# Layer 3's token layer: gate weights without their mean, and tokens scaled by the identity that transposes them

## The chip, the cores and the metric

The kernel runs on one core of one Trainium2 chip. The metric is the device time of one execution in microseconds; three executions of the kernel before gave 7714.85 (median), 7708.21 and 7727.53. The engines are named as in the profile: PE (TensorE matmul), PEld (TensorE weight load), DVE (VectorE), ACT (ScalarE), POOL (GpSimd) and SP (SyncE, which issues DMAs).

## The reference

Four layers run one after the other on an array of 8 images of 56x56 pixels with 128 channels: a deformable convolution block, a whitening, and two token layers, each an attention and a mixture of experts. Only the way into the experts of layer 3 (the fourth) matters here. It takes the tokens after the linear attention, 3136 per image, normalizes each over its 128 channels, multiplies by 64 rows of gate weights, and picks for every expert the eight tokens with the highest softmax over the tokens:

```python
def _ln_t(v, eps=1e-5):
    m = jnp.mean(v, axis=-1, keepdims=True)
    s = jnp.var(v, axis=-1, keepdims=True)
    return (v - m) / jnp.sqrt(s + eps)
...
t = t + _L3_attn_ref(_ln_t(t), L3_attn_w_in, L3_attn_w_out, L3_attn_b_out, L3_attn_ln_w)
t = t + _L3_ffn_ref(_ln_t(t), L3_ffn_gate_w, L3_ffn_gate_b, L3_ffn_weight1, L3_ffn_weight2)
...
# in _L3_ffn_ref
logits = jnp.einsum('bsd,ed->bse', x, gate_w) + gate_b
probs = jax.nn.softmax(logits, axis=1)
vals, idx = jax.lax.top_k(probs.transpose(0, 2, 1), K)
```

## The kernel before

The layers follow each other in one program. Nearly all of the span belongs to the convolution, the whitening and layer 2's attention. Layer 3 has three parts: `context_sums` (a pass over all tokens for the attention's key sums), `linear_layer` (the rest of the attention, the gate and the choice of tokens) and `run_experts`. The change is in `linear_layer` and in `gate_weights`, which prepares the gate weights of layers 2 and 3 once, when the token layers begin.

**Tiling.** `linear_layer` cuts an image into 7 groups (NG) of 4 x 112 tokens (GT = 4, T = 112; QC = 448 tokens). Tokens lie on 112 partitions, 4 x 128 channels behind each other. A group is a Python generator, and each `yield` ends one of its stages. `pipeline` starts a new group each turn and advances every group in flight by one stage, so one turn holds one stage each of about ten different groups. There are 8 x 7 = 56 groups. Within a turn, a scheduler of the language settles the order of the instructions on each engine; every engine then works its own queue in order and waits where a semaphore says so.

**Stages of a group**, with the lines: load xT by DMA on SP (L2084); p_q = xT times w_in on PE (L2088) and its exponential q on ACT (L2101); sum m and reciprocal on DVE (L2103, L2104), q times m on POOL (L2105); transpose of q on PE (L121) and copy qT on ACT (L122); p_y on PE (L2112), its squares with sums sq on ACT (L2118), rs on DVE (L2122) and the power -1/2 on POOL (L2123); y on DVE (L2126) and t = t + y on POOL (L2129); then the normalization for the gate, which the change touches:

- `group_stats`: statistics and their aggregation on DVE (L1975, L1976), rs in `rsqrt`: add eps on DVE (L1140), power -1/2 on POOL (L1141);
- `minus_mean`: ms = -mean times rs on DVE (L1983); `scale_shift`: xn = t times rs + ms, four instructions on ACT (L1990);
- with the last group of an image, t goes to `t_c` and to the output by two DMAs on SP (L2138);
- `transpose_group`: four transposes of xn into PSUM tile p_tr on PE (L121), and a copy to nT on ACT (L122);
- p_g = gate weights times nT on PE (L2144), and pr = p_g + bias on ACT (L2145).

After an image's last group, `choose` goes on in the same generator: the top 8 of each row on DVE (L1650, L1653), exponentials on ACT (L1663), p_take on PE (L1679), four gathers from `t_c` issued on POOL (L1711), their statistics and p_pool (L1697 to L1706). These run in the turns of the next image's groups.

The identity `k.ident` is a constant 128x128 tile. A transpose takes the tile with the data as weights and the identity as the moving operand.

Of the kernel before, what the change touches and what calls it, by code (L numbers as in the profile page):

```python
# [8 lines left out]
F32 = mybir.dt.float32  # L9
# [3 lines left out]
ALU = mybir.AluOpType  # L13
AX = mybir.AxisListType
# [3 lines left out]
NB, IH, IW, C = 8, 56, 56, 128  # L18
S = IH * IW
T = 112  # L20
NT = S // T
GT = 4
# [24 lines left out]
E, HID, EG = 64, 512, 4  # L47
# [69 lines left out]
def transpose_group(nc, k, ps, tag, dst, src, copy):  # L117

    p = ps.tile([128, GT, T], F32, tag=tag, name="p_tr")
    for i in range(GT):  # L120
        nc.tensor.transpose(p[:, i, :], src[:, i, :], k.ident[:T, :T])  # L121
    copy(dst, p.rearrange("p a b -> p (a b)"))  # L122
# [889 lines left out]
def load_tokens(nc, dst, src):  # L1012

    nc.sync.dma_start(dst, src.rearrange("(t p) c -> p t c", p=T))
# [121 lines left out]
def rsqrt(nc, k, pool, mv, n):  # L1136

    m = mv.shape[0]
    rs = pool.tile([m, n], F32, name="rs")
    nc.vector.tensor_scalar(rs, mv[:, :, 1], EPS, None, ALU.add)  # L1140
    nc.gpsimd.tensor_tensor(rs, rs, k.mhalf[:m, :n], ALU.pow)  # L1141
    return rs
# [748 lines left out]
def pipeline(starts, every):  # L1891


    flight = []
    turn = 0
    starts = list(starts)
    while starts or flight:
        if starts and turn % every == 0:
            flight.append(starts.pop(0))
        advance(flight, len(flight))  # L1900
        turn += 1
# [68 lines left out]
def group_stats(nc, k, pool, x):  # L1970

    st = pool.tile([T, GT, 6], F32, name="st")
    mv = pool.tile([T, GT, 2], F32, name="mv")
    for i in range(GT):
        nc.vector.bn_stats(st[:, i], x[:, i])  # L1975
        nc.vector.bn_aggr(mv[:, i], st[:, i])  # L1976
    return rsqrt(nc, k, pool, mv, GT), mv


def minus_mean(nc, pool, rs, mv):  # L1980

    ms = pool.tile([T, GT], F32, name="ms")
    nc.vector.scalar_tensor_tensor(ms, mv[:, :, 0], -1.0, rs, ALU.mult, ALU.mult)  # L1983
    return ms


def scale_shift(nc, out, x, rs, ms):

    for i in range(GT):
        nc.scalar.activation(  # L1990
            out[:, i], x[:, i], AF.Identity, bias=ms[:, i : i + 1], scale=rs[:, i : i + 1]
        )
# [70 lines left out]
def linear_layer(tc, k, w, low, cw, t_in, xT_in, t_out, out, gate_w, gate_b, taken, pooled):  # L2063


    nc = tc.nc
    n_b = pooled.shape[1]
    G = GT * H3
    with ExitStack() as ctx:
        bp = ctx.enter_context(tc.tile_pool(name="llb", bufs=2))  # L2070
        wp = ctx.enter_context(tc.tile_pool(name="llw", bufs=3))
        ps = ctx.enter_context(tc.tile_pool(name="llp", bufs=8, space=PSUM))
        st_of = {}

        def group(n, g):
            if g == 0:
                t = bp.tile([T, NT, C], F32, name="t")
                load_tokens(nc, t, t_in[n])
                pr = bp.tile([E, S], F32, name="pr")
                st_of[n] = t, pr  # L2080
            t, pr = st_of[n]
            t = t[:, g * GT : (g + 1) * GT]
            xT = wp.tile([C, QC], F32, name="xT")
            nc.sync.dma_start(xT, xT_in[n][:, g * QC : (g + 1) * QC])  # L2084
            yield
            p = ps.tile([T, GT, C], F32, tag="m", name="p_q")
            for i in range(GT):
                nc.tensor.matmul(  # L2088
                    p[:, i], xT[:, i * T : (i + 1) * T], w.w_in[:, :C], start=True, stop=True
                )  # L2090
            q = wp.tile([T, GT, C], F32, name="q")
            q3 = q.rearrange("p a (h d) -> p (a h) d", d=D3)
            m = wp.tile([T, G], F32, name="m")
            mb = m.unsqueeze(2).to_broadcast([T, G, D3])
            if low is None:
                p3 = p.rearrange("p a (h d) -> p (a h) d", d=D3)
                nc.vector.tensor_reduce(m, p3, AX.X, ALU.max)
                nc.vector.tensor_tensor(q3, p3, mb, ALU.subtract)
                nc.scalar.activation(q, q, AF.Exp)
            else:  # L2100
                nc.scalar.activation(q, p, AF.Exp, bias=low[:T])  # L2101
            yield
            nc.vector.tensor_reduce(m, q3, AX.X, ALU.add)  # L2103
            nc.vector.reciprocal(m, m)  # L2104
            nc.gpsimd.tensor_tensor(q3, q3, mb, ALU.mult)  # L2105
            yield
            qT = wp.tile([C, QC], F32, name="qT")
            transpose_group(nc, k, ps, "m", qT, q, nc.scalar.copy)
            yield
            p = ps.tile([T, GT, C], F32, tag="m", name="p_y")  # L2110
            for i in range(GT):
                nc.tensor.matmul(  # L2112
                    p[:, i], qT[:, i * T : (i + 1) * T], cw, start=True, stop=True
                )
            y = wp.tile([T, GT, C], F32, name="y")
            sq = wp.tile([T, GT], F32, name="sq")
            for i in range(GT):
                nc.scalar.activation(  # L2118
                    y[:, i], p[:, i], AF.Square, accum_out=sq[:, i : i + 1]
                )  # L2120
            rs = wp.tile([T, GT], F32, name="rs")
            nc.vector.tensor_scalar(rs, sq, 1.0 / C, EPS, ALU.mult, ALU.add)  # L2122
            nc.gpsimd.tensor_tensor(rs, rs, k.mhalf[:T, :GT], ALU.pow)  # L2123
            yield
            for i in range(GT):
                nc.vector.scalar_tensor_tensor(  # L2126
                    y[:, i], p[:, i], rs[:, i : i + 1], w.ln_w, ALU.mult, ALU.mult
                )
            nc.gpsimd.tensor_tensor(t, t, y, ALU.add)  # L2129
            yield  # L2130
            rs, mv = group_stats(nc, k, wp, t)
            yield
            ms = minus_mean(nc, wp, rs, mv)
            xn = wp.tile([T, GT, C], F32, name="xn")
            scale_shift(nc, xn, t, rs, ms)
            if g == NG - 1:
                for d in (t_out[n], out[n]):
                    nc.sync.dma_start(d.rearrange("(t p) c -> p t c", p=T), st_of[n][0])  # L2138
            yield
            nT = wp.tile([C, QC], F32, name="nT")  # L2140
            transpose_group(nc, k, ps, "m", nT, xn, nc.scalar.copy)
            yield
            p = ps.tile([E, QC], F32, tag="m", name="p_g")
            nc.tensor.matmul(p, gate_w, nT, start=True, stop=True)  # L2144
            nc.scalar.activation(  # L2145
                pr[:, g * QC : (g + 1) * QC], p, AF.Identity, bias=gate_b
            )
            if g == NG - 1:
                yield from choose(nc, k, wp, ps, pr, t_out[n], taken[:, n], pooled[:, n])

        pipeline([group(n, g) for n in range(n_b) for g in range(NG)], 1)


# [11 lines left out]


def gate_weights(nc, k, pool, rp, ps, gate_w, gate_b, name):
    raw = rp.tile([E, C], F32, name=name + "_raw")
    nc.sync.dma_start(raw, gate_w)
    p = ps.tile([C, E], F32, tag="tr", name="p_tr")  # L2170
    nc.tensor.transpose(p, raw, k.ident[:E, :E])
    t = pool.tile([C, E], F32, name=name)
    nc.vector.tensor_copy(t, p)
    b = pool.tile([E, 1], F32, name=name + "_b")
    with nc.allow_non_contiguous_dma(reason="one bias on each partition"):
        nc.sync.dma_start(b, gate_b.unsqueeze(1))
    return t, b


def token_layers(tc, k, a, y, out):  # L2180
# [3 lines left out]
    with ExitStack() as ctx:  # L2184
# [13 lines left out]
        with tc.tile_pool(name="tlr", bufs=1) as rp:  # L2198
            with tc.tile_pool(name="tlp", bufs=2, space=PSUM) as ps:
# [10 lines left out]
                for g in range(2):  # L2210
# [12 lines left out]
                w.w_out = transposed(nc, k, cp, rp, ps, a["L3_attn_w_out"], "w_out")  # L2223
                gates = [
                    gate_weights(
                        nc, k, cp, rp, ps, a[f"L{i}_ffn_gate_w"], a[f"L{i}_ffn_gate_b"], f"gate{i}"
                    )
# [116 lines left out]
```

## Time and profile before

| | |
|---|---|
| three executions | 7708.21, 7714.85, 7727.53 us |
| profiled execution, own time | 7718.14 us |
| its span on the core | 7716.3 us |
| mean granted TensorE clock | 0.90 |
| first and last t = t + y in `linear_layer` (start) | 7059.2 and 7435.5 us |
| busy in 7060 to 7440 us: PE, DVE, ACT, POOL | 259.0, 297.7, 283.9, 264.0 of 380 us |

The span is the time between the first and the last instruction on the core in the profiled execution; the time of the execution is 1.8 us longer. In the profile's lines a group of instructions is written as line, engine, operation, output<-inputs, shapes and count. In a timeline, each row has the start and the length in us; the brackets give the idle time of the engine just before, and what ended it. Times inside the span count from its start.

### The profile page before, as it was taken

To read this page: it belongs to the slowest core of one execution; us is meant where nothing else is said; L and a number is where in the kernel's file an instruction comes from. 1 tells how busy PE (TensorE), PEld (TensorE's weight loads), DVE (VectorE), ACT (ScalarE), POOL (GpSimd) and SP (SyncE) were. 2 spreads that over 40 slices of the span, in tenths; PEclk is the share of its full clock that TensorE was granted. 3 is DMA by queue.
4 is the path that set the end of the run, shared out by engine and by line. 5 is a ranking of instruction groups with operands and counts; after the bars stand their busy time and mean duration, and the time that the engine had idled before them with its cause. 6 is when DMAs were issued, how large, how long until landed. Compare 5 with 4: busy or idle time off the path is not lost. (4 is left out here: it accounts for less than half of the span.)

```text
span 7716.3 us, 157926 instructions
## 1 busy us (share of the span) xinstructions
PE 6482.3 (84%) x59883; PEld 2880.7 (37%) x59883; DVE 5284.8 (68%) x9856; ACT 4142.6 (54%) x6467; POOL 2935.1 (38%) x2555
## 2 busy tenths in 40 slices
PE   6659999556899999999999999999999997556654
PEld 4446666334233323323323323333333333245532
DVE  7975564366677777777777777777777776366752
ACT  4424444122666666666666666666666664056740
POOL 0011111022444444444444444444444443434653
PEclk8768898777999999999999999999999998788766
DMA  5453443376788778778778778778778775543543
GB/s 155 137 119 76 86 95 65 82 240 207 199 203 197 193 192 199 189 192 201 191 184 204 188 183 207 183 191 205 185 190 206 182 190 137 196 117 107 134 135 130
DMA packets 736303, 1287.38 MB, mean 167 GB/s; under 512 B 117698, under 2 KB 503108, under 8 KB 728516
## 3 DMA queue, kind: packets, MB, share of 16 engines
q1 hardware_dynamic: 725556, 1260.76, 65.1%
q0 software_dynamic: 6144, 12.60, 0.6%
q8 instruction: 484, 7.93, 0.5%
q10 hardware_dynamic: 3824, 3.68, 0.2%
q14 instruction: 295, 2.42, 0.1%
HBM read 286.04 MB, written 197.81 MB: 63 GB/s over the span
## 5 line engine op out<-in xcount | busy, mean ns | idle before, releaser
L1260 ACT ACTIVATE e<-p_s 128x768 f32<-128x768 f32 (+2 forms) x3712 | 2887.8, 830 | 1584.9 <-PE p_s L1252 1329.8
L1298 POOL COPY x<-sq 32x1152 f32<-32x1152 f32 x1792 | 2059.2, 1149 | 2067.6 <-PE p_s L1252 1330.0
L1271 DVE STREAM_TRANSPOSE sq<-e 128x768 f32<-128x768 f32 x2688 | 2434.5, 950 | 567.3 <-ACT e L1260 312.9
L1252 PE MATMUL p_s<-q,kT 32*128 32x384 f32 (+2 forms) x14848 | 1888.6, 548 | 33.6 <-ACT e L1260 18.6
L1305 PE MATMUL av<-e,va 128*32 128x384 f32 (+2 forms) x14848 | 1645.3, 515 | 30.4 <-DVE acc L1324 20.7
L1305 PE MATMUL avx<-x,va 128*32 128x384 f32 x10752 | 1138.3, 496 | 69.5 <-issue 40.2
L1252 PEld LDWEIGHTS p_s<-q,kT 32*128 32x128 f32 (+1 forms) x14848 | 654.8, 181 | 1252.6 <-issue 825.4
L1305 PEld LDWEIGHTS av<-e,va 128*32 128x32 f32 (+1 forms) x14848 | 294.5, 108 | 1049.4 <-issue 941.7
L1305 PEld LDWEIGHTS avx<-x,va 128*32 128x32 f32 x10752 | 353.2, 111 | 650.9 <-issue 595.2
L609 POOL TENSOR_TENSOR rs<-rs,mhalf 112x4 f32<-112x4 f32 x112 | 116.1, 1036 | 788.3 <-DVE rs L608 788.3
L1324 DVE TENSOR_TENSOR acc<-acc,avx 128x384 f32<-128x384 f32 x336 | 183.9, 547 | 229.9 <-PE avx L1305 228.6
L121 PE MATMUL p_tr<-ident,xn 112*128 112x112 f32 x672 | 134.6, 341 | 187.4 <-DVE xn L112 141.8
L1141 POOL TENSOR_TENSOR rs<-rs,mhalf 112x4 f32<-112x4 f32 (+2 forms) x136 | 168.1, 1236 | 269.3 <-DVE ntop L1942 123.8
L525 ACT COPY wT<-p_w 88x448 f32<-88x448 f32 x152 | 138.0, 922 | 194.1 <-PE p_w L523 161.4
L1990 ACT ACTIVATE xn<-t,ms,rs 112x128 f32<-112x128 f32 x448 | 185.3, 488 | 76.4 <-DVE ms L1983 76.4
L327 DVE SCALAR_TENSOR_TENSOR acc<-xp,dw,acc 128x3136 f32<-128x3136 f32 x56 | 194.3, 3478 | 31.3 <-ACT acc L322 31.2
L637 PE MATMUL p_f<-x1T,w 128*128 128x448 f32 x448 | 205.6, 583 | 4.4 <-DVE x1T L632 2.7
L121 PEld LDWEIGHTS p_tr<-ident,xn 112*128 112x128 f32 x672 | 98.7, 169 | 285.0 <-issue 185.1
L1385 POOL TENSOR_TENSOR rs<-rs,mhalf 128x3 f32<-128x3 f32 (+1 forms) x72 | 58.5, 815 | 365.0 <-DVE rs L1384 343.0
L523 PE MATMUL p_w<-ident,wide 112*88 112x112 f32 x896 | 146.5, 303 | 58.6 <-DMA px<-strips 34.1
L621 DVE TENSOR_TENSOR y<-y,p_rs 128x448 f32<-128x448 f32 x112 | 69.3, 619 | 176.6 <-PE p_rs L614 176.6
L122 ACT COPY xT<-p_tr 128x448 f32<-128x448 f32 x112 | 59.6, 532 | 229.8 <-PE p_tr L121 203.7
(354 smaller groups left out, 7830.9 us busy)
## 6 DMA issues: line engine op xcount, KB each, us to landing
x<-sq SPq DMA_DIRECT2D x5376, 144.0 KB
w<-in_L_ffn_weight_dram SPq DMA_DIRECT2D x64, 1024.0 KB
px<-strips SPq DMA_DIRECT2D x64, 616.0 KB
va_d<-va SPq DMA_DIRECT2D x16, 1600.0 KB
xT_d<-xT SPq DMA_DIRECT2D x112, 224.0 KB
xT<-xT_d SPq DMA_DIRECT2D x112, 224.0 KB
kT_d<-kT SPq DMA_DIRECT2D x16, 1568.0 KB
t<-t_a SPq DMA_DIRECT2D x16, 1568.0 KB
```

The source lines that it names most:

```text
L121: nc.tensor.transpose(p[:, i, :], src[:, i, :], k.ident[:T, :T])
L327: nc.vector.scalar_tensor_tensor(acc, xp[:, j // 3 : j // 3 + IH, j % 3 : j % 3 + IW], dw[:, j : j + 1], acc, ALU.mult, ALU.add,)
L523: nc.tensor.transpose(p[:, g], around[:, :, g], k.ident[:T, :T])
L637: nc.tensor.matmul(p, q.w1[:, f * 128 : (f + 1) * 128], x1T, start=True, stop=True)
L1141: nc.gpsimd.tensor_tensor(rs, rs, k.mhalf[:m, :n], ALU.pow)
L1252: nc.tensor.matmul(ss[j // 2][:m, j % 2, :width], kT[rows, 128 * i : 128 * i + m], q[rows, :width], start=True, stop=True,)
L1260: nc.scalar.activation(e[:m, 2 * j : 2 * j + 2, :width], ss[j][:m, :, :width], AF.Exp)
L1271: nc.vector.transpose(sq[:, :, i, j : j + 2].rearrange("p s j c -> p j s c"), exps[u, b, a, i][:, j : j + 2, :QB].rearrange("p j (s c) -> ...
L1298: nc.gpsimd.tensor_copy(*moves.pop(0))
L1305: nc.tensor.matmul(out, keys[u, b][1][:m, i, j, :], e[j], start=start, stop=stop)
L1324: nc.vector.tensor_tensor(to, to, in_order(av), ALU.add)
L1990: nc.scalar.activation(out[:, i], x[:, i], AF.Identity, bias=ms[:, i : i + 1], scale=rs[:, i : i + 1])
```

## The change

The normalized token is rs (t - mean). Its product with a gate row does not change when the mean of the gate row over the channels is taken off first, since the token without its mean sums to zero; and then the mean of the token need not be subtracted any more. So the gate rows lose their mean once, in `gate_weights` (for both layers), and in `linear_layer` xn is gone: the scale rs goes into the identity, as a diagonal tile `own` of 4 x 112 x 112, and a matmul of t with it scales and transposes at once. ms and xn are not computed any more; `own` is made on POOL; the four transposes become four ordinary matmuls with the weights t and the moving operand `own`, into p_n in place of p_tr. The DMAs of the last group move one stage up, and the number of stages stays as it was, by an empty `yield`.

```diff
             nc.gpsimd.tensor_tensor(t, t, y, ALU.add)
             yield
-            rs, mv = group_stats(nc, k, wp, t)
-            yield
-            ms = minus_mean(nc, wp, rs, mv)
-            xn = wp.tile([T, GT, C], F32, name="xn")
-            scale_shift(nc, xn, t, rs, ms)
+
+            rs, _ = group_stats(nc, k, wp, t)
+            own = wp.tile([T, GT, T], F32, name="own")
+            nc.gpsimd.tensor_tensor(
+                own,
+                k.ident[:T, :T].unsqueeze(1).to_broadcast([T, GT, T]),
+                rs.unsqueeze(2).to_broadcast([T, GT, T]),
+                ALU.mult,
+            )
             if g == NG - 1:
                 for d in (t_out[n], out[n]):
                     nc.sync.dma_start(d.rearrange("(t p) c -> p t c", p=T), st_of[n][0])
             yield
+            yield
             nT = wp.tile([C, QC], F32, name="nT")
-            transpose_group(nc, k, ps, "m", nT, xn, nc.scalar.copy)
+            p = ps.tile([C, GT, T], F32, tag="m", name="p_n")
+            for i in range(GT):
+                nc.tensor.matmul(p[:, i], t[:, i], own[:, i], start=True, stop=True)
+            nc.scalar.copy(nT, p.rearrange("p a b -> p (a b)"))
             yield
             p = ps.tile([E, QC], F32, tag="m", name="p_g")
             nc.tensor.matmul(p, gate_w, nT, start=True, stop=True)
...
     raw = rp.tile([E, C], F32, name=name + "_raw")
     nc.sync.dma_start(raw, gate_w)
+    mean = rp.tile([E, 1], F32, name=name + "_m")
+    nc.vector.tensor_reduce(mean, raw, AX.X, ALU.add)
+    nc.vector.tensor_scalar(mean, mean, 1.0 / C, None, ALU.mult)
+    nc.vector.tensor_scalar(raw, raw, mean, None, ALU.subtract)
     p = ps.tile([C, E], F32, tag="tr", name="p_tr")
     nc.tensor.transpose(p, raw, k.ident[:E, :E])
```

## The prediction

> **What bounds the kernel now.** I read the page's engine totals first.
>
> ```profile
> PE 6482.3 (84%) x59883; PEld 2880.7 (37%) x59883; DVE 5284.8 (68%) x9856; ACT 4142.6 (54%) x6467; POOL 2935.1 (38%) x2555
> ```
>
> POOL looks like the emptiest engine, but this is a mean over stages with different limits; almost all of the span is not touched by the change. So I went to the stage that is: `linear_layer` adds its 56 groups into t (L2129) from 7059.2 to 7435.5 us. The busy times by stretch of it (length; then PE, PEld, DVE, ACT, POOL busy and instructions; clock; DMA):
>
> ```profile
> 7060.00:7440.00 380.00, 259.01 (x1440) 189.21 (x1440) 297.66 (x1088) 283.92 (x963) 263.96 (x249) 0.80 0.46 121
> 7084.98:7090.35 5.37, 3.78 (x28) 2.74 (x28) 4.23 (x18) 4.91 (x17) 4.32 (x4) 1.00 0.15 44
> 7212.59:7223.30 10.71, 4.15 (x22) 3.95 (x22) 10.70 (x25) 4.97 (x17) 4.65 (x5) 0.66 0.02 6
> 7246.44:7257.21 10.77, 7.96 (x37) 5.74 (x38) 5.24 (x23) 7.18 (x27) 8.22 (x9) 0.68 0.87 227
> ```
>
> Here no engine is far from the others: a plain turn (row two), a turn with the top-8 search (three), one with the gathers (four). What closes a plain turn stands in POOL's timeline (start, length, idle before and who ended it):
>
> ```profile
> 7084.98 1.28 POOL L2129 TENSOR_TENSOR t<-t,y 112x512 f32<-112x512 f32 x1 [0.26 <-DVE y L2126]
> 7086.88 1.05 POOL L2105 TENSOR_TENSOR q<-q,m 112x512 f32<-112x512 f32 x1 [0.62 <-ACT xn L1990]
> 7088.10 1.02 POOL L2123 TENSOR_TENSOR rs<-rs,mhalf 112x4 f32<-112x4 f32 x1 [0.17 <-DVE rs L1140]
> 7089.09 1.01 POOL L1141 TENSOR_TENSOR rs<-rs,mhalf 112x4 f32<-112x4 f32 x1
> 7090.35 1.27 POOL L2129 TENSOR_TENSOR t<-t,y 112x512 f32<-112x512 f32 x1 [0.26 <-DVE y L2126]
> ```
>
> and DVE's, over the same turn:
>
> ```profile
> 7085.41 0.87 DVE L1983 SCALAR_TENSOR_TENSOR ms<-mv,rs 112x4 f32<-112x4 f32 x1
> 7086.29 0.29 DVE L1975 BATCH_NORM_STATS2 st<-t 112x6 f32<-112x128 f32 x1
> 7086.50 0.24 DVE L2104 RECIPROCAL m<-m 112x16 f32<-112x16 f32 x1
> ...
> 7087.56 0.39 DVE L2122 TENSOR_SCALAR rs<-sq 112x4 f32<-112x4 f32 x1
> 7087.87 0.16 DVE L1140 TENSOR_SCALAR rs<-mv 112x4 f32<-112x4 f32 x1
> 7089.15 1.13 DVE L2126 SCALAR_TENSOR_TENSOR y<-p_y,rs,ln_w 112x128 f32<-112x128 f32 x4 [1.13 <-POOL rs L2123]
> ```
>
> The loop is POOL t, DVE statistics of t, DVE reciprocal, POOL q, DVE rs, POOL rs, DVE y, POOL t: 5.37 us, of it POOL idle 0.26 + 0.62 + 0.17. Two readings matter. The 0.62 is put down to ACT, but the reciprocal that q needs ends at 7086.74, 0.14 before q starts, and it stands in DVE's queue behind the statistics, which need t. And ms takes 0.87 where the same line takes 0.16 in `context_sums` (6941.24): it starts at 7085.41 and ends 0.02 after POOL's t, so it sits out POOL's add; L2122 ends at 7087.95 with POOL's q (7087.93) likewise. ACT is not in the loop: xn waits for ms, and nothing in the loop waits for xn.
>
> Other turns are pure POOL, back to back, 4.40 us:
>
> ```profile
> 7066.18 1.02 POOL L2123 TENSOR_TENSOR rs<-rs,mhalf 112x4 f32<-112x4 f32 x1
> 7067.17 1.05 POOL L2105 TENSOR_TENSOR q<-q,m 112x512 f32<-112x512 f32 x1
> 7068.39 1.01 POOL L1141 TENSOR_TENSOR rs<-rs,mhalf 112x4 f32<-112x4 f32 x1 [0.17 <-DVE rs L1140]
> 7069.36 1.27 POOL L2129 TENSOR_TENSOR t<-t,y 112x512 f32<-112x512 f32 x1
> ```
>
> I sorted the 55 intervals between the adds by length: 9 near 4.4, 22 near 5.36, 7 near 10.4 (search), 6 near 10.8 (gathers), 11 mixed, of 6.1 to 8.4; together 376.3 us.
>
> **The change, part by part.** *ACT* loses four xn of L1990 per group, 1.65 us a turn; *DVE* loses ms, 0.87. Both are covered in the plain loop: the statistics behind ms wait for t in any case, which ends when ms does. I count no gain there.
>
> *PE* gets four ordinary matmuls for four transposes. In the trace a transpose is one record and a matmul two: four transposes into p_tr take 0.60, eight records of p_y 1.04, so at most 0.44 a turn at full clock and 0.9 at half. Cover: PE waits 1.59 us for q in a plain turn, and p_y, behind the new matmuls, feeds ACT's y, which now need not wait for 1.65 us of xn. Without cover it would be 55 x 0.44 = 24 us.
>
> *POOL* gets `own`, 56 multiplications of 112x448. No row has that shape. Bounds: at the rate alone of L1117 (128x3200 in 5.518 us, 1.72 ns an element) 0.77; the add L2129 as it stands, 1.26. Nearest is L2105, also a multiplication with one operand spread over the inner dimension: 1.05 less 64 elements at 1.72 ns is 0.94, which I take.
>
> The Trainium skill ("GPSIMD Engine Reference", section Elementwise — side-by-side cycle accounting) gives some 2.6 cycles an element at 1.2 GHz for two inputs; my estimate from it is 0.97, and the sum below would be 1 us higher. Its section Engine selection speaks against the change: it puts elementwise multiplication on VectorE, about twice as fast. The trace agrees only in part: DVE's `own` L1742, 128x512, takes 0.68 against POOL's 1.05.
>
> Where `own` stands: the built order has it directly behind L1141 and ahead of the next t in nearly every turn. Queued behind it is the add, on it the statistics, the reciprocal and q. In a plain turn the 0.26 before t goes, since y (1.13) is hidden under L1141 and `own` (0.97 + 0.94): 5.37 - 0.26 + 0.94 = 6.05, or +0.68. The 0.62 stays, for the reciprocal still stands behind the first statistics.
>
> - 9 POOL turns: +0.94 each, 8.5.
> - 22 plain turns: +0.68, 15.0.
> - 7 search turns: DVE is busy throughout (10.70 of 10.71), yet L1141 at the end releases t, and `own` comes between. Between -0.15 (ms there) and +0.94; the middle, +0.4: 2.8.
> - 6 gather turns: POOL's order of four gathers, rs, rs, t; +0.68: 4.1.
> - 11 mixed turns: between -0.87 (ms) and +0.68 plus; PE and DVE wait for the search's results, so I take little, +0.2: 2.2.
>
> Sum +32.6. *SP:* t_c and out are issued a turn earlier, past one xT load at most; PE waited 2.8 us in all for xT from 7060 to 7440. The earlier wait for the add is queued ahead of xT loads that have three buffers. Zero; without cover, those few us. *`gate_weights`:* six small DVE operations for both layers, at most 0.29 each (the copy of w_out), 1.7 us, with the PE transposes and DVE copies behind them. The cover is the load of t:
>
> ```profile
> 1602.02 0.48 DVE L1067 BATCH_NORM_STATS2 st<-t 112x6 f32<-112x128 f32 x2 [7.90 <-DMA t<-y]
> ```
>
> The profiled execution took 7718.14 (span 7716.3, 1.8 around it); with +32.6 it is 7750.7. It lies 3.3 above the median 7714.85, from which I forecast 7748.
>
> Ends: with 0.77 for `own` and the lower ends of search and mixed turns, 6.9 + 11.2 - 1.1 + 3.1 - 9.6 = +11; with 1.26 everywhere, 9 x 1.26 + 22 x 1.0 + 7 x 1.26 + 17 x 1.0 = +59.
>
> **Rivals.** *Hidden:* POOL is idle 116 of 380 us, and 56 x 0.94 = 53 fits. If the scheduler's new order closes the 0.62 gaps too, 22 plain turns cost 0.06 each and the sum is 32.6 - 13.6 = 19: 7734. Against it: the statistics remain ahead of the reciprocal.
>
> *POOL holds DVE more:* each `own` stops DVE's rs (L1140, L2122) as t stops ms now, and is as slow as an add: 7715 + 59 = 7774. For it: the 0.87. Against: ms itself is gone.
>
> *The long turns win:* in the 24 long turns DVE and ACT lie on the path, and each gets shorter by ms and xn, 0.87 + 1.65 = 2.5: -60, with +23.5 for the short ones -37: 7678. It decides from 1.0 us per long turn on (23.5 / 24). For it: DVE full in the search turns. Against: ms is only 0.15 there, and POOL's 8.22 of 10.77 with the gathers.
>
> **How the numbers follow.** A measurement of this kernel (7708.21 to 7727.53 unchanged) tells about 0.3%, 23 us. Forecast (+18 to +45) 0.60, hidden 0.17, holding 0.15, long turns 0.08. Slower by over 23: most of the forecast and all of holding, 0.68; the rest of the forecast, hidden and a part of the long turns, same 0.25; faster 0.07. The range leaves out the last rival and the top of the third: 7718 to 7772.
>
> **What would show it.** `own` near 0.94 with t directly behind it; plain turns near 6.05, POOL turns near 5.35; POOL's busy share in the stage above 0.8; ACT idle up. Wrong if q follows t without a gap, if `own` is under 0.6, or if the turns with search and gathers shrink by over 1 us.

## The result

| | median | lowest to highest | runs |
|---|---|---|---|
| kernel before | 7713.92 us | 7695.88 to 7727.53 | 11 |
| changed kernel | 7750.43 us | 7736.87 to 7763.54 | 11 |

The ratio is 1.0049, with a 95% interval of 1.004 to 1.0057: the change costs some 36 us. The profiled execution of the changed kernel took 7752.65 us (span 7750.6). Its engine totals, the first line of the page:

```profile
PE 6512.0 (84%) x60107; PEld 2913.0 (38%) x60107; DVE 5246.1 (68%) x9806; ACT 4067.8 (52%) x6243; POOL 2985.9 (39%) x2611
```

POOL gained 56 instructions and 50.8 us of busy time, ACT lost 224 instructions and 74.8 us, DVE lost 38.7 us; PE has 29.7 us more. One engine got more work and two got less, and the kernel is slower: the totals don't say why. So again the stage, from the first to the last start of t = t + y (L2129): 412.1 us, where it was 376.3. These +35.8 us agree with the 36.5 between the medians, so the rest of the program needs no look. Busy time by stretch (length; then PE, PEld, DVE, ACT, POOL with instructions; clock; DMA):

```profile
7060.00:7470.00 410.00, 285.42 (x1644) 218.88 (x1644) 251.93 (x1027) 211.76 (x747) 311.01 (x302) 0.81 0.42 110
7100.61:7106.61 6.00, 3.36 (x17) 2.83 (x16) 3.45 (x16) 1.98 (x11) 5.19 (x6) 0.68 1.00 273
7118.62:7130.81 12.19, 4.91 (x26) 3.79 (x25) 10.51 (x23) 2.92 (x12) 5.23 (x6) 0.69 0.13 36
```

POOL is busy for 311.0 of 410 us (0.76; before 264.0 of 380, 0.69), and DVE and ACT have fallen far behind it (0.61 and 0.52). The clock granted in the stage is what it was, 0.81 against 0.80. The second row is a plain turn, the third a turn that holds both long steps of a search (DVE busy for 10.51 of 12.19 us). Now POOL and DVE in that plain turn, from the timeline of all engines (start, length, idle before and what ended it):

```profile
7100.61 1.26 POOL L2129 TENSOR_TENSOR t<-t,y 112x512 f32<-112x512 f32 x1
7101.91 0.29 DVE L1975 BATCH_NORM_STATS2 st<-t 112x6 f32<-112x128 f32 x1 [2.31 <-POOL t L2129]
7102.12 0.23 DVE L2104 RECIPROCAL m<-m 112x16 f32<-112x16 f32 x1
...
7102.50 1.05 POOL L2105 TENSOR_TENSOR q<-q,m 112x512 f32<-112x512 f32 x1 [0.62 <-DVE mv L1976]
...
7103.65 1.02 POOL L2123 TENSOR_TENSOR rs<-rs,mhalf 112x4 f32<-112x4 f32 x1
7104.64 1.01 POOL L1141 TENSOR_TENSOR rs<-rs,mhalf 112x4 f32<-112x4 f32 x1
7104.70 1.12 DVE L2126 SCALAR_TENSOR_TENSOR y<-p_y,rs,ln_w 112x128 f32<-112x128 f32 x4 [1.06 <-POOL rs L2123]
7105.72 0.93 POOL L2134 TENSOR_TENSOR own<-ident,rs 112x448 f32<-112x448 f32 x1
7106.61 1.26 POOL L2129 TENSOR_TENSOR t<-t,y 112x512 f32<-112x512 f32 x1
```

Read it from the bottom. The next t (7106.61) follows `own` directly; y had been ready since 7105.82, so the old gap of 0.26 is gone and `own` sets the start. The 0.62 ahead of q is still there, because the reciprocal still stands behind the first statistics, and those wait for t. The turn is 6.00 us long, where it was 5.37. In the groups (count, then busy us and mean ns of one, then idle before), the first line is of the kernel before, from 7060 to 7440 us, the others of the changed kernel, whole execution:

```profile
L2129 POOL TENSOR_TENSOR t<-t,y 112x512 f32<-112x512 f32 x56 | 70.8, 1264 | 10.9 <-DVE y L2126 9.3 <-PE p_tr L121 1.3 <-DVE rs L1701 0.3
```

```profile
L2129 POOL TENSOR_TENSOR t<-t,y 112x512 f32<-112x512 f32 x56 | 70.8, 1265 | 3.2 <-DVE rs L2122 1.8 <-PE p_tr L121 1.3
...
L2134 POOL TENSOR_TENSOR own<-ident,rs 112x448 f32<-112x448 f32 x56 | 52.2, 932 | 4.1
```

`own` takes 0.932 us, 52.2 in all. POOL idles only 3.2 us ahead of the 56 adds and never for DVE's y, for which it idled 9.3 us before: nearly always the add waits for POOL itself. The turn shown is the one that was predicted, but not the commonest: only two of the 21 plain turns of the table below take 6.00. The others stand in the part on why the prediction was right.

### The profile page after: what moved, and what is told of

It is laid out like the page before. It is cut to its first block, busy times and chain, and to the rows that moved or that the text cites. A ratio compares the mean times of both kernels' runs of the same rounds, so it can differ in the third digit from the quotient of the medians.

```text
span 7750.6 us, 158188 instructions
## 1 busy us (share of the span) xinstructions
PE 6512.0 (84%) x60107; PEld 2913.0 (38%) x60107; DVE 5246.1 (68%) x9806; ACT 4067.8 (52%) x6243; POOL 2985.9 (39%) x2611
## 3 DMA queue, kind: packets, MB, share of 16 engines
q14 instruction: 295, 2.41, 0.1%
## 5 line engine op out<-in xcount | busy, mean ns | idle before, releaser
L1305 PE MATMUL av<-e,va 128*32 128x384 f32 (+2 forms) x14848 | 1644.4, 515 | 30.5 <-DVE acc L1324 20.7
L1141 POOL TENSOR_TENSOR rs<-rs,mhalf 112x4 f32<-112x4 f32 (+2 forms) x136 | 167.6, 1234 | 299.2 <-DVE rs L1140 130.4
L121 PE MATMUL p_tr<-ident,xn 112*128 112x112 f32 x448 | 91.8, 350 | 184.0 <-DVE xn L112 140.4
L327 DVE SCALAR_TENSOR_TENSOR acc<-xp,dw,acc 128x3136 f32<-128x3136 f32 x56 | 194.2, 3477 | 29.7 <-ACT acc L322 29.6
L1975 DVE BATCH_NORM_STATS2 st<-t 112x6 f32<-112x128 f32 x448 | 114.5, 276 | 101.6 <-POOL t L2129 100.5
L642 PE MATMUL p_f<-hid,w 128*128 128x448 f32 x448 | 180.2, 545 | 0.2 <-issue 0.2
```

What stands on the lines that cost most here:

```text
L327: nc.vector.scalar_tensor_tensor(acc, xp[:, j // 3 : j // 3 + IH, j % 3 : j % 3 + IW], dw[:, j : j + 1], acc, ALU.mult, ALU.add,)
L642: nc.tensor.matmul(p[:, :QC], q.w2[:, f], hid[:, f], start=(f == 0), stop=(f == 3))
L1305: nc.tensor.matmul(out, keys[u, b][1][:m, i, j, :], e[j], start=start, stop=stop)
```

## The experiments

The measure is the length of the stage from the first to the last start of the 56 adds, split by kinds of turn as in the prediction; each of the 55 intervals keeps the kind it had in the kernel before. One thing is counted otherwise: a search can spread over two turns, so each of the 7 search turns is taken together with the turn ahead of it (6 of the mixed and 1 of the plain ones), which leaves 21 plain and 5 mixed turns. The stage is a finer measure than the time, as the rest of the program varies: the first add starts between 7047.7 and 7072.1 us in the 14 profiled executions. But each stage is read from one execution. e8, whose edit lies outside the stage, came out 2.3 us below the kernel before, 2.1 of it in the mixed turns, so differences of some 3 us say nothing. The ratio is to runs of the kernel before on the same chip. In the diffs of the experiments the operands are written short, and only the lines that matter are given.

| kernel | stage | 9 POOL | 21 plain | 7 + 7 search | 6 gather | 5 mixed | median, ratio [95%] |
|---|---|---|---|---|---|---|---|
| before | 376.3 | 39.4 | 113.1 | 119.8 | 64.9 | 39.1 | 7713.92 |
| changed | 412.1 | 48.4 | 131.9 | 124.5 | 62.8 | 44.5 | 7750.43, 1.0049 [1.004, 1.0057] |
| e1 | 355.1 | 43.0 | 111.7 | 106.9 | 58.8 | 34.7 | 7707.34, 0.9982 [0.9971, 0.9993] |
| e2 | 361.6 | 39.4 | 112.8 | 117.2 | 61.6 | 30.5 | 7712.68, 0.9984 [0.9975, 0.9994] |
| e3 | 405.4 | 47.8 | 123.1 | 122.5 | 66.8 | 45.2 | 7757.07, 1.0039 [1.0027, 1.0051] |
| e4 | 358.7 | 39.4 | 112.9 | 110.1 | 60.2 | 36.1 | 7712.6, 0.9988 [0.998, 0.9997] |
| e5 | 391.7 | 48.4 | 122.8 | 119.7 | 58.6 | 42.2 | 7732.42, 1.0018 [1.0007, 1.0029] |
| e6 | 343.4 | 39.4 | 105.9 | 104.6 | 58.1 | 35.4 | 7695.03, 0.9966 [0.9953, 0.9979] |
| e7 | 429.9 | 55.9 | 143.4 | 131.6 | 61.8 | 37.2 | 7772.42, 1.007 [1.0053, 1.0086] |
| e8 | 374.0 | 39.4 | 113.1 | 119.7 | 64.7 | 37.0 | 7723.69, 1.0005 [0.9994, 1.0017] |
| e9 | 373.4 | 39.4 | 113.8 | 120.2 | 64.7 | 35.3 | 7712.02, 0.9999 [0.9988, 1.001] |
| e10 | 352.2 | 39.4 | 108.2 | 109.6 | 62.8 | 32.1 | 7689.71, 0.997 [0.9959, 0.9981] |
| e11 | 345.2 | 39.4 | 92.3 | 124.9 | 56.0 | 32.6 | 7683.07, 0.9963 [0.9951, 0.9975] |
| e12 | 336.7 | 43.5 | 105.3 | 105.6 | 57.9 | 24.5 | 7687.21, 0.9959 [0.9946, 0.9972] |

The kernel before stood at 7726.15 beside e1 to e4, at 7718.76 beside e5 to e8 and at 7711.96 beside e9 to e12.

### Where `own` is made: e1, e2, e3, e4

e1 makes `own` on DVE, one stage later:

```diff
-            nc.gpsimd.tensor_tensor(own, ident, rs, ALU.mult)
             yield
+            nc.vector.tensor_tensor(own, ident, rs, ALU.mult)
```

> The changed kernel with the multiplication that makes own on DVE, one stage later, in place of POOL; the four matmuls per group and the gate weights stay. Theory A (the 0.93 us of POOL per turn, queued ahead of t = t + y, is what the change costs): POOL has four instructions a turn again, plain turns go back to 5.4 us, the adds of the stage take 345 to 376 us in place of 412, and the time is 7685 to 7715. Theory B (the doubled PE work of the matmuls costs it): nothing of PE is changed, the stage stays at about 412 us and the time at 7750. Theory C (DVE pays as POOL did, since a DVE instruction here sits out POOL's add): the multiplication takes 0.9 to 1.3 us each and the time is 7730 to 7760.

The stage became 355.1 us, 57.0 shorter than the changed kernel's and 21.2 shorter than that of the kernel before. Theory A's numbers hold; theory C was right about the length of the multiplication, 1.151 us, and wrong about its price. DVE's part is dearer than its other rows: from L1742, at 0.68 for 512 elements, 0.60 would be my estimate for 448. Group and timeline of e1:

```profile
L2138 DVE TENSOR_TENSOR own<-ident,rs 112x448 f32<-112x448 f32 x55 | 63.3, 1151 | 24.8 <-POOL rs L1141 24.5
```

```profile
7089.29 1.27 POOL L2129 TENSOR_TENSOR t<-t,y 112x512 f32<-112x512 f32 x1
7089.36 1.69 DVE L2138 TENSOR_TENSOR own<-ident,rs 112x448 f32<-112x448 f32 x1
...
7090.52 1.40 POOL L2123 TENSOR_TENSOR rs<-rs,mhalf 112x4 f32<-112x4 f32 x1
```

DVE's `own` starts during POOL's add and ends 0.49 after it, and POOL's power behind it takes 1.40 instead of 1.02: the two engines stop each other. That held the gain down (the POOL turns are at 43.0, where they were at 39.4 before) but did not take it.

e2 makes `own` on ACT, in four instructions, also one stage later:

```diff
-            nc.gpsimd.tensor_tensor(own, ident, rs, ALU.mult)
             yield
+            for i in range(GT):
+                nc.scalar.activation(own[:, i], ident, AF.Identity, scale=rs[:, i:i+1])
```

> The changed kernel with own made on ACT, by four instructions per group that scale the identity by rs, where the four xn of L1990 were. Theory A: ACT does as before the change, POOL too, only ms is gone; plain turns 5.4 us, the stage 355 to 376 us, the time 7695 to 7715. Theory B (PE's matmuls): 412 us and 7750.

The stage is 361.6 us. The POOL and plain turns are back at 39.4 and 112.8, where the kernel before has them, and the mixed turns are shorter than there by 8.6. This is what the account with POOL's queue expects of a stage without `own` on POOL. Both e1 and e2 also move `own` one stage later. A run with `own` on POOL one stage later was not made, so what a better place in POOL's own queue would give is not known.

e3 puts `own` alone into the kernel before, and nothing reads it:

```diff
             rs, mv = group_stats(nc, k, wp, t)
+            own = wp.tile([T, GT, T], F32, name="own")
+            nc.gpsimd.tensor_tensor(own, ident, rs, ALU.mult)
             yield
             ms = minus_mean(nc, wp, rs, mv)
```

> The kernel before, with POOL's multiplication added behind L1141 into a tile that nothing reads; xn, ms, transposes and gate weights are as before. Theory A: the whole cost of the change comes back, plain turns of 6.0 us and POOL turns of 5.4, the stage 405 to 412 us, the time 7745 to 7755. Theory B (PE's matmuls): the stage stays at 376 us and the time at 7714.

The stage grew by 29.1, the time by 30.9 against the kernel before on that chip. The plain turn of 6.00 came out, in 13 of the 21, with everything that the change removes still in place. Theory A's turns are met, but not "the whole cost": 29.1 is less than 35.8. POOL in e3's timeline:

```profile
7104.27 1.05 POOL L2105 TENSOR_TENSOR q<-q,m 112x512 f32<-112x512 f32 x1 [0.62 <-DVE mv L1976]
...
7107.49 0.93 POOL L2133 TENSOR_TENSOR own<-ident,rs 112x448 f32<-112x448 f32 x1
7108.39 1.27 POOL L2129 TENSOR_TENSOR t<-t,y 112x512 f32<-112x512 f32 x1
```

From 7102.39, the start of the add before, to 7108.39 it is 6.00 us. So the instruction alone lengthens the loop, by the step that was predicted (0.63 against 0.68).

e4 is the changed kernel without `own`: its matmuls multiply t by the plain identity, so the scaling by rs is left out.

```diff
-            nc.gpsimd.tensor_tensor(own, ident, rs, ALU.mult)
...
-                nc.tensor.matmul(p[:, i], t[:, i], own[:, i], ...)
+                nc.tensor.matmul(p[:, i], t[:, i], ident, ...)
```

> The changed kernel without own: the four matmuls take the plain identity, so the scaling of the tokens by rs before the gate is left out, and other tokens are chosen; rs (L1140, L1141) is still computed. Theory A: with POOL's multiplication gone the stage is at or under the 376 us of before, 355 to 376, and the time 7695 to 7715. Theory B (PE's matmuls): all eight matmul records per group are still there, so 400 to 412 us and 7740 to 7750.

The stage is 358.7 us: without `own` it is 53.4 shorter, as theory A has it. In the kernel before the same instruction cost 29.1. Both can't be the price of one thing, unless what it displaces differs. And e4 lies 17.6 below the kernel before: what the change removes is worth something after all. The next runs take that apart.

### What the removed work and the matmuls are worth: e5, e6, e9, e10

e5 keeps `own` but transposes t as before (so the scaling is left out again); e6 has neither `own` nor the matmuls:

```diff
-                nc.tensor.matmul(p[:, i], t[:, i], own[:, i], ...)
+                nc.tensor.transpose(p[:, i], t[:, i], ident)
```

> The changed kernel, own still made on POOL but read by nothing: four transposes of t with the plain identity in place of the four matmuls, so the scaling of the tokens before the gate is left out and other tokens are chosen. It takes PE's 0.44 us a turn away alone. Theory A (POOL's multiplication in the queue is the cost, PE is covered): the stage stays at 405 to 412 us and the time at 7745 to 7752. Theory B (the matmuls cost their own part, directly or by the order that the scheduler makes of them): the stage falls to 385 to 395 us and the time to 7725 to 7735.

> As the run without own (scaling left out, plain identity), but with transposes in place of the matmuls: neither POOL's nor PE's addition is left, and ms and xn are gone. Theory A: within 5 us of the run with the matmuls, a stage of 354 to 359 us, a time of 7705 to 7713. Theory B: 10 to 20 us less, a stage of 340 to 349 us and a time of 7692 to 7702.

The stages are 391.7 and 343.4 us. Theory A, with nothing for the matmuls, missed both, and theory B's numbers hold: the matmuls in place of transposes cost 20.4 (391.7 to 412.1) with `own` there and 15.3 (343.4 to 358.7) without. The two also tell more of `own`. From e6 to e5 it costs 48.3, though nothing reads it there, so the wait of the matmuls for it is not what makes it dearer than in e3. The same figures read the other way: beside `own` the removals are worth less, 13.7 (e3 to e5) where they give 32.9 without it (before to e6).

The price of the matmuls is spread over all kinds but the POOL turns; with `own` there, 9.1 of it lie in the plain ones. One of those begins at 7312.61 in the changed kernel and at 7303.03 in e5, and takes 7.11 and 5.93 us. POOL of the changed kernel, with one line of DVE:

```profile
7312.61 1.27 POOL L2129 TENSOR_TENSOR t<-t,y 112x512 f32<-112x512 f32 x1
...
7314.51 1.05 POOL L2105 TENSOR_TENSOR q<-q,m 112x512 f32<-112x512 f32 x1 [0.62 <-DVE tot L1674]
7314.56 1.02 DVE L1675 TENSOR_SCALAR found<-found,tot 64x8 f32<-64x8 f32 x1
...
7315.80 1.02 POOL L2123 TENSOR_TENSOR rs<-rs,mhalf 112x4 f32<-112x4 f32 x1 [0.24 <-DVE rs L2122]
...
7317.74 1.01 POOL L1141 TENSOR_TENSOR rs<-rs,mhalf 112x4 f32<-112x4 f32 x1 [0.93 <-PE p_q L2088]
...
7318.83 0.93 POOL L2134 TENSOR_TENSOR own<-ident,rs 112x448 f32<-112x448 f32 x1
```

and of e5:

```profile
7303.03 1.27 POOL L2129 TENSOR_TENSOR t<-t,y 112x512 f32<-112x512 f32 x1
...
7304.78 1.02 POOL L2123 TENSOR_TENSOR rs<-rs,mhalf 112x4 f32<-112x4 f32 x1 [0.47 <-DVE rs L2122]
...
7305.05 0.20 DVE L1675 TENSOR_SCALAR found<-found,tot 64x8 f32<-64x8 f32 x1
...
7305.77 1.05 POOL L2105 TENSOR_TENSOR q<-q,m 112x512 f32<-112x512 f32 x1
...
7306.98 1.01 POOL L1141 TENSOR_TENSOR rs<-rs,mhalf 112x4 f32<-112x4 f32 x1 [0.17 <-DVE rs L1140]
...
7308.07 0.93 POOL L2134 TENSOR_TENSOR own<-ident,rs 112x448 f32<-112x448 f32 x1
```

The work is the same, the order is not: e5 has rs for y (L2123) ahead of q and idles 0.47 + 0.17, the changed kernel has q first and idles 0.62 + 0.24 + 0.93. (The 0.93 is put down to PE, but L1141 raises DVE's rs of L1140 to its power, and that rs ends at 7317.60, 0.14 before, behind the first half of y.) The order also settles what POOL holds up on DVE: `found`, a step of the search, takes 1.02 us beside q in the changed kernel, where it ends 0.02 after q, and 0.20 beside the power in e5; DVE's two rs stand behind it. In this turn it is an order in queues, not time on PE. e9 tests whether PE's time costs anything in the order of before: the kernel before, with matmuls by the identity for its four transposes, and nothing else.

```diff
-            transpose_group(nc, k, ps, "m", nT, xn, nc.scalar.copy)
+            for i in range(GT):
+                nc.tensor.matmul(p[:, i], xn[:, i], ident, start=True, stop=True)
+            nc.scalar.copy(nT, p)
```

> The kernel before with four ordinary matmuls of xn with the identity in place of its four transposes; ms, xn and the gate weights are as before. Theory A (in the order of before, PE's extra 0.44 us a turn lies under its wait for q, and the 15 and 20 us of the runs with and without matmuls come with the orders that the scheduler made there): the stage stays at 374 to 380 us, the time at 7714 to 7722. Theory B (the matmuls cost PE time wherever they stand): a stage of 388 to 398 us, a time of 7727 to 7737.

The stage is 373.4 us (0.6 under theory A's range, within the scatter) and the ratio 0.9999. PE's groups, over the stage of the kernel before, of e9 and of the changed kernel (7060 to 7470 us):

```profile
L121 PE MATMUL p_tr<-ident,xn 112*128 112x112 f32 x212 | 40.1, 322 | 0.1
L121 PE MATMUL p_tr<-ident,q 112*128 112x112 f32 x212 | 37.5, 310 | 75.8 <-POOL q L2105 75.8
```

```profile
L2143 PE MATMUL p_n<-ident,xn 112*128 112x112 f32 x424 | 70.5, 317 | 0.0
...
L121 PE MATMUL p_tr<-ident,q 112*128 112x112 f32 x212 | 35.8, 300 | 71.2 <-POOL q L2105 71.0
```

```profile
L121 PE MATMUL p_tr<-ident,q 112*128 112x112 f32 x212 | 38.0, 312 | 96.9 <-POOL q L2105 96.8
```

The matmuls of e9 occupy PE for 70.5 us, where the transposes of xn took 40.1, and PE's wait for q shrank from 75.8 to 71.2. In the order of before, PE's extra work is covered, as predicted. In the changed kernel PE waits 96.9 us for q, so it is not short of time there either. So what the matmuls cost beside the other edits, 15 to 20 us, is put down to the order that comes with them. That is argued, not shown: the turn above is one case, and why the scheduler orders so was not followed up.

e10 is the kernel before without ms: ACT scales t by rs alone, and the gate weights lose their mean as in the changed kernel.

```diff
-            ms = minus_mean(nc, wp, rs, mv)
...
-            scale_shift(nc, xn, t, rs, ms)
+            for i in range(GT):
+                nc.scalar.activation(xn[:, i], t[:, i], AF.Identity, scale=rs[:, i:i+1])
```

> The kernel before with gate weights without mean, and xn = t times rs by the same four ACT instructions per group but without the shift, so that only ms on DVE is gone; transposes as before. It splits what the removals gave (stage 343 us without ms and xn). If ms on DVE gave it: a stage of 343 to 356 us and a time of 7690 to 7703. If xn on ACT gave it: 365 to 376 us and 7705 to 7717.

The stage is 352.2 us: without ms, 0.87 us on DVE in a queue that waits for POOL anyway, it is 24.1 shorter. Of that, 10.2 came in the searches with the turns ahead of them and 7.0 in the mixed turns. Not all of it belongs to ms: without the shift, ACT's four xn are shorter too, 1.28 us in place of 1.65, which the expectation does not count. One turn ahead of a search is 7.50 long before (from 7205.09) and 5.17 in e10 (from 7194.21). The timeline of all engines, of the kernel before:

```profile
7205.52 0.85 DVE L1983 SCALAR_TENSOR_TENSOR ms<-mv,rs 112x4 f32<-112x4 f32 x1
...
7206.40 1.65 ACT L1990 ACTIVATE xn<-t,ms,rs 112x128 f32<-112x128 f32 x4 [1.22 <-DVE ms L1983]
...
7207.96 0.25 ACT L2118 ACTIVATE y<-p_y 112x128 f32<-112x128 f32 x1
...
7208.86 0.20 ACT L2118 ACTIVATION_READ_ACCUMULATOR y<-p_y 112x1 f32 x1
...
7210.05 0.14 DVE L2122 TENSOR_SCALAR rs<-sq 112x4 f32<-112x4 f32 x1
...
7210.34 1.02 POOL L2123 TENSOR_TENSOR rs<-rs,mhalf 112x4 f32<-112x4 f32 x1 [2.32 <-DVE rs L1140]
```

and of e10:

```profile
7194.33 1.28 ACT L2135 ACTIVATE xn<-t,rs 112x128 f32<-112x128 f32 x4
...
7195.51 0.27 ACT L2118 ACTIVATE y<-p_y 112x128 f32<-112x128 f32 x1
...
7196.41 0.21 ACT L2118 ACTIVATION_READ_ACCUMULATOR y<-p_y 112x1 f32 x1
...
7196.82 0.15 DVE L2122 TENSOR_SCALAR rs<-sq 112x4 f32<-112x4 f32 x1
...
7197.12 1.02 POOL L2123 TENSOR_TENSOR rs<-rs,mhalf 112x4 f32<-112x4 f32 x1 [0.64 <-DVE cmv L1698]
```

Before, ms sits out POOL's add until 7206.37, xn waits for ms, the squares of y (L2118) and the reading of their sums stand behind xn on ACT, and DVE's rs and POOL's power wait for the sums. Follow the sums from the start of the turn: they were ready after 3.97 us (7209.06), and without ms after 2.41 (7196.62). Of these 1.56 us, 1.19 come from the start of xn, which lies 1.31 into the turn in the kernel before and 0.12 in e10, and 0.37 from the shorter xn. The rest of the 2.33, some 0.8, is the order on DVE: before, its rs stood another 0.99 us behind statistics of chosen tokens, which waited for a DMA; in e10 it stood 0.20 behind others. So the chain through xn is shown in this turn, and how the 24.1 divides over ms, the shorter xn and the order is not.

### The rest: e7, e8, e11, e12

e7 adds to the changed kernel a second multiplication like `own`, into a tile that nothing reads.

```diff
             nc.gpsimd.tensor_tensor(own, ident, rs, ALU.mult)
+            more = wp.tile([T, GT, T], F32, name="more")
+            nc.gpsimd.tensor_tensor(more, ident, rs, ALU.mult)
```

> The changed kernel with the multiplication on POOL made twice per group, the second into a tile that nothing reads. Theory A: POOL is on the path in nearly all turns, so a second 0.93 us costs nearly its full sum of 55 x 0.93 = 51 us as the first did against the run without own (53): a stage of 455 to 465 us, a time of 7790 to 7802. Rival (the first one cost by the order it caused, POOL still has idle time to give): 430 to 445 us and 7768 to 7783.

The stage is 429.9 us and the time 7772.42: theory A missed, and the rival's numbers come out (the stage 0.1 below its range). The second multiplication cost 17.8 us where the first cost 53.4. POOL of e7:

```profile
7072.42 1.02 POOL L2123 TENSOR_TENSOR rs<-rs,mhalf 112x4 f32<-112x4 f32 x1
7073.41 1.05 POOL L2105 TENSOR_TENSOR q<-q,m 112x512 f32<-112x512 f32 x1
7074.56 1.01 POOL L1141 TENSOR_TENSOR rs<-rs,mhalf 112x4 f32<-112x4 f32 x1
7075.64 0.93 POOL L2134 TENSOR_TENSOR own<-ident,rs 112x448 f32<-112x448 f32 x1
7076.53 0.93 POOL L2141 TENSOR_TENSOR more<-ident,rs 112x448 f32<-112x448 f32 x1
7077.43 1.27 POOL L2129 TENSOR_TENSOR t<-t,y 112x512 f32<-112x512 f32 x1
```

This is one of the POOL turns. From add to add it is 6.24 us (7071.19 to 7077.43), back to back, where the changed kernel had 5.40, with 0.17 idle: here the second multiplication costs nearly its length, 0.84. The 9 POOL turns pay 7.5 us in all. The 21 plain turns pay 11.5, or 0.55 each, so part of it falls into waits that POOL still had; the mixed turns are 7.3 shorter, in another order. The price of one and the same instruction was 18, 29 and 53 us in three surroundings.

e8 makes only the change to the gate weights, in the kernel before:

```diff
+    mean = rp.tile([E, 1], F32, name=name + "_m")
+    nc.vector.tensor_reduce(mean, raw, AX.X, ALU.add)
+    nc.vector.tensor_scalar(mean, mean, 1.0 / C, None, ALU.mult)
+    nc.vector.tensor_scalar(raw, raw, mean, None, ALU.subtract)
```

> The kernel before with the gate rows' mean taken off, and nothing else. Theory A (the six DVE instructions lie under the wait for the load of t): no difference that can be measured, 7714 within 8, ratio 0.999 to 1.001; DVE waits some 7 us for the load where it waited 7.9. Rival (they hold up the transposes of the setup): up to 2 us, which only the timeline can show.

The ratio is 1.0005 and its interval reaches across 1, so no difference can be measured. The six instructions take up part of the wait that was to cover them. DVE in e8:

```profile
1600.86 0.48 DVE L1067 BATCH_NORM_STATS2 st<-t 112x6 f32<-112x128 f32 x2 [6.50 <-DMA t<-y]
```

It waits 6.50 us for the load of t, 1.40 less than before.

e11 and e12 look for a better kernel: e2 and e1 with one more `yield`, so that rs for y (L2122, L2123) comes a stage later.

```diff
+            yield
             rs = wp.tile([T, GT], F32, name="rs")
```

> As the run with own on ACT, and with rs of the attention's normalization (L2122, L2123) one stage later, so that it is ready at the head of a turn and need not stand behind the statistics of t. If the loop through the statistics, q, rs, y sets the plain turns (5.37 us), they fall to POOL's own 4.4: a stage of 335 to 350 us, a time of 7690 to 7705. If not, the stage stays at 360 us and the time at 7712.

> As the run with own on DVE (stage 355 us), and with rs one stage later as well. If that loop sets the plain turns: a stage of 325 to 345 us, a time of 7685 to 7700. If DVE's and POOL's stops of each other set them (own 1.15 us on DVE, rs 1.40 on POOL there): 350 to 360 us and 7705 to 7712.

The stages are 345.2 and 336.7 us. Both kernels are faster than both that were compared, by little: 0.9963 [0.9951, 0.9975] and 0.9959 [0.9946, 0.9972] of the kernel before, and e10 with 0.997 is level with them within the intervals. In e12 the stage is 39.6 us shorter than before and the time only 24.8, so not all that the stage gains is gained by the program. In e11 the plain loop is broken: plain turns are 4.40 on average (92.3 / 21), with POOL back to back in most, but the searches grew from 117.2 in e2 to 124.9. In e12 the searches are short (105.6) and the plain turns 5.01, with POOL's power at 1.40 in several of them, as in e1.

## Why the prediction was right, and where it was not

The time, +36.5 in the medians against the predicted +33, was right, and so was the main mechanism: `own` stands in POOL's queue ahead of the add, and the add now waits for POOL. That the sum comes out so closely is partly luck, because errors of opposite sign cancel. The stage can be walked in four steps, each from a run:

| step | stage | 9 POOL | 21 plain | 7 + 7 search | 6 gather | 5 mixed | sum |
|---|---|---|---|---|---|---|---|
| ms gone, xn shorter (before to e10) | 376.3 to 352.2 | 0 | -4.9 | -10.2 | -2.1 | -7.0 | -24.1 |
| xn gone, DMAs moved (to e6) | to 343.4 | 0 | -2.3 | -5.0 | -4.7 | +3.3 | -8.8 |
| matmuls for transposes (to e4) | to 358.7 | 0 | +7.0 | +5.5 | +2.1 | +0.7 | +15.3 |
| `own` on POOL (to changed) | to 412.1 | +9.0 | +19.0 | +14.4 | +2.6 | +8.4 | +53.4 |
| all | | +9.0 | +18.8 | +4.7 | -2.1 | +5.4 | +35.8 |
| predicted, in these columns | | +8.5 | +14.3 | +4.7 | +4.1 | +1.0 | +32.6 |

(The prediction's 22 x 0.68 and 11 x 0.2 are divided here as 21 x 0.68 and 5 x 0.2, the rest with its searches.) In another order the steps have other sizes (`own` before the matmuls is +48.3, the matmuls +20.4): they are not independent, and by the scatter of some 3 us the small entries mean little.

- *The size of `own`*: it takes 0.932 us, against the 0.94 taken from the nearest row. The estimate from the Trainium skill ("GPSIMD Engine Reference", section Elementwise — side-by-side cycle accounting), 0.97, lies 0.04 above it.
- *Its place*: directly behind L1141 and ahead of t, as predicted. POOL turns take 5.38 on average (5.35 predicted), the 0.26 is gone, and e3 shows the plain turn of 6.00 alone (6.05 predicted). In the changed kernel itself the step "The 0.62 stays" holds in part. Two of the 21 plain turns take 6.00. Three take 5.40 or 5.41: there rs for y stands ahead of q, and the 0.62 has closed. Eight take 6.76 to 7.11: the 0.62 is there, and POOL waits another 0.87 to 0.93 ahead of L1141. Five take 6.17 to 6.32: POOL has no gap but a power more, for the chosen tokens. The last three take 5.25, 5.71 and 5.92. The mean is 6.28, and the kind came out at +18.8 instead of +14.3.
- *POOL's busy share*, to be above 0.8, is 0.76. It could not be above 0.8 by the prediction's own numbers: 264.0 us and 56 x 0.94 are 316.6, which is 0.77 of 380 + 32.6.
- *"I count no gain there"*, for ms and xn: this step failed. It was argued from the plain loop, where it nearly holds (-4.9 over 21 turns), and carried over to the other turns, apart from lower ends of -0.15 and -0.87 for the search and mixed turns. In turns like the one shown from e10, "nothing in the loop waits for xn" is false: the squares of y stand behind xn in ACT's queue. The runs give -24.1 for the step without ms and with a shorter xn, and -8.8 for the rest of xn with the moved DMAs.
- *PE*: in the order of before it is covered by its wait for q, as e9 shows. The price that came with the matmuls beside the other edits, 15 to 20 us, was in no case of the prediction.
- *The kinds with many waits*: +4.7 for the searches with the turns ahead of them is met to the tenth by luck: it is +14.4 for `own`, +5.5 for the matmuls and -15.2 for the removals, not a small price for each. The gather turns went down 2.1 instead of up 4.1: `own` cost 2.6 there and the matmuls 2.1, and the removals gave 6.8.
- *Gate weights*: nothing, by e8. *SP*: not tried by itself; PE waits for no xT in the changed kernel's stage, where it waited 2.8 us before.
- *The rivals*: "hidden" had a condition, that the new order closes the 0.62, and it came true in three plain turns; but POOL did not hide `own`, since without it there the stage is 50.5 (e2) and 53.4 (e4) shorter. "POOL holds DVE more" was priced at +59. DVE's two rs (L2122 and L1140) together take 28.7 us in the stage where they took 26.1, so the hold is there, but it is small. "The long turns win" was partly true: without ms, xn and `own` (e6) the 25 turns of the last three kinds go from 223.8 to 198.1, 1.03 each, which is just the point from which that rival was to decide, and less than half of its 2.5. In the changed kernel `own` and the new order take all of it back (231.8), which the rival priced at nothing.

## What to carry to other kernels

Where several engines form a loop with a wait in each, the removal of an instruction is not worth nothing because its engine waits anyway: follow what stands behind it in its own queue, in every kind of turn and not only in the commonest. Moving work to the engine with the lowest total is judged at the place where it is queued: one multiplication cost 18, 29 or 53 us in three surroundings, and putting it on DVE or ACT one stage later made the same algorithm slightly faster than both kernels (0.9982 and 0.9984, with rs later 0.9959 and 0.9963). And when a sum comes out right, check its parts: here -33, +15 and +53 stood behind a forecast of 0, 0 and +33.

## What the runs showed of the hardware

The time that a tiny DVE instruction takes depends on POOL: ms, on 112x4, takes 0.16 us alone and 0.85 to 0.87 beside POOL's add. e1 shows it in both directions: DVE's multiplication takes 1.69 during the add (1.151 on average, 0.58 at its shortest), and POOL's power behind it 1.40 instead of 1.02. The Trainium skill ("SBUF — State Buffer", section Who interferes with whom) says that a DVE instruction with two SBUF inputs contends with a GpSimd instruction that reads SBUF, that the ports they share are locked exclusively, and that the order of issue decides who is blocked. These rows agree: ms ends with POOL's add, and POOL's power of e1 ends late behind DVE's multiplication. In "GPSIMD Engine Reference", section Engine selection, VectorE is about twice as fast for such a multiplication; here its mean was 1.151 against POOL's 0.932. So the advice held in the stage's length (355.1 against 412.1, with `own` also one stage later) and not in the mean duration of the instruction.

POOL's power on 112x4 takes 1.01 us, more than `own` on 112x448: the two powers of a turn cost POOL as much as its two largest multiplications.
